# Four gated cross-attention layers with experts: the fourth attention's order of work, its inverse root and its norm

## The chip, the cores and the metric

The kernel runs on one core of a Trainium2 chip, as one launch. The metric is the device time of one execution in microseconds (us). The engines that matter here are TensorE (PE in the profile; its weight loads are PEld), VectorE (DVE), ScalarE (ACT) and GpSimd (POOL); SyncE (SP) issues most of the transfers, GpSimd those whose addresses are computed.

## The reference

The residual x is 16 x 128 rows ("blocks" of 128 tokens) of 256 numbers. Four times it goes through a cross-attention to a context of 128 rows a block and through a feed-forward layer, each behind a layer norm and added back through a gate. All is float32. The change is mostly in the fourth attention, which is followed by the fourth feed-forward layer, a mixture of experts with 8 experts a token:

```python
x = x + jnp.tanh(g_xattn[3]) * _L3_xattn_ref(_layernorm(x, axis=-1), ctx_1024, ...)
x = x + jnp.tanh(g_ffn[3]) * _L3_ffn_ref(_layernorm(x, axis=-1), L3_ffn_router_weight, ...)

# _L3_xattn_ref, 16 heads of 16, EPS = 1e-06, y = context, DCA = 16
y_dca = y[:, -DCA:, :]
y_main = y[:, :-DCA, :]
kv_dca = (y_dca @ Wkv_dca + bkv_dca).reshape(b, DCA, 2, H, HD)
k_dca = _ln(kv_dca[:, :, 0], kn_dca_w, kn_dca_b)
q = _ln((x @ Wq + bq).reshape(b, s1, H, HD), qn_w, qn_b)
k = _ln(kv[..., :HD], kn_w, kn_b)          # kv from y_main
ctx = _attn(qT, k, v)                      # softmax over 112 keys
ctx_dca = _attn(qT, k_dca, v_dca)          # softmax over 16 keys
return (ctx + ctx_dca) @ Wo + bo
```

`_ln` divides each head's 16 deviations from the mean by the root of their variance plus 1e-6: for a block of 128 tokens that is one inverse root for each token, each of the 16 heads, and q and k, an array of 128 x 32. The fourth mixture sends each token to its 8 best of 64 experts; an expert takes the first 128 tokens sent to it.

## The kernel before

Eight stages run one after the other over x, which stays in SBUF as `x_sb`: xattn0, ffn0, xattn1, ffn1, xattn2, ffn2, xattn3, ffn3. The last pair, xattn3 and ffn3, is block 4.

**xattn3.** A step handles one block b of 128 tokens; step n of the loop does the scores and exponentials of block n, the sums and values of block n-1, the output projection of block n-2, and prepares blocks n+2 and n+3. The pieces of a step are these, with the lines in the profile.

- `project_qk` (L1261 to L1265): queries and keys of a block into one PSUM bank; VectorE adds the bias. The weights have had each head's mean taken out, so the results are deviations already. `squares` (L1269) squares them on ScalarE.
- `normalise_qk` (L1273 to L1278): VectorE sums the squares of each head into v (128 x 32), divides by 16 and adds 1e-6; `inverse_root` (L392 to L401) finds 1/sqrt(v) on VectorE from a shifted-integer guess and three Newton steps; GpSimd multiplies q and k by it.
- `turn_qk` (L1287 to L1300): TensorE transposes q and k, ScalarE copies them out with the norm's weights (qT, kT).
- `scores` and `maxima` (L1315, L1327): products of q and k into the four "sc" banks, then eight VectorE reduces that write the negative maximum of each part of the keys beside the queries. `with_maxima` transposes and copies the queries again (qT), and `exponentials` (L1315, L1340) forms the products the other way round, the maximum already taken off, and applies Exp on ScalarE, four times.
- `project_v` (L1345 to L1348): values, on TensorE and ScalarE.
- `add_up` and `values` (L1358, L1364): TensorE sums the exponentials and weights the values; VectorE takes the reciprocal rd of the sums.
- `quotients` (L1376 to L1381): TensorE spreads rd over a bank, ScalarE copies it (rs), VectorE multiplies (aT).
- `project` (L1387, L1388, L410): four matmuls and a fifth with a row of ones for the bias; VectorE adds the gated result to x.

PSUM gives four banks to "sc", two to "tr" (transposes, sums, rd's spread and the router's logits), one to "av" and one to "pj" (both projections).

**The norm and the additions before it.** The rows that the third mixture of experts returned (yg) are added to x block by block (`settle`, L287, four additions a block). `norm_steps` puts the work of a group of four blocks at fixed steps: the four additions-to-x of blocks from eight steps ahead, then statistics (L427 to L430), 1/sqrt on GpSimd (L385), the normalised rows (L442) and their transposition (L455, L463). The first group is done ahead of the loop (`layernorm`).

**The router of the fourth mixture.** The object `head` gets a `done(b)` for each block that leaves `project`, and after each pair of blocks it lays out a list of pieces, one for each following tick; a step has two ticks, one after `quotients` and one at its end. The pieces are: norm statistics, rows, transposition, logits (L158 to L166), the 8 largest (L171 to L176), chosen experts and their weights (L185 to L204), places in the experts' rows (L212), targets (L222 to L234), and then the sends (L240), 16 a pair of blocks, by which GpSimd scatters the rows hx to the experts' buffer `xs_f`, one transfer for each of the 8 choices of each block. `finish`, at the head of ffn3, runs what is left. ffn3 then loads the rows of each expert (xe, L1447), transposes them (L761), and computes.

**What sets the order.** In xattn3 the instructions of TensorE, VectorE and ScalarE run in the order in which the code issues them (`manual_schedule`); those of GpSimd and the transfer queues are ordered by the framework's scheduler. Each engine executes in order, so an instruction that waits holds back all behind it on that engine. The other stages leave all engines to the scheduler, except where they too write the order out. The loop, before:

```python
for b in range(B + 2):
    normalise_qk(b + 2); scores(b); maxima(b, first of 4 banks)
    add_up(b - 1); values(b - 1); maxima(b, other banks)
    project(b - 2); quotients(b - 1)
    tick(done=b - 2)
    with_maxima(b); project_qk(b + 3); exponentials(b); project_v(b)
    squares(b + 3); turn_qk(b + 2); norm work of step b
    tick()
```

Of the kernel before, what the change touches and what calls it, by code (L numbers as in the profile page):

```python
# [28 lines left out]
P = 128  # L29
# [62 lines left out]
class Routed:  # L92
# [30 lines left out]
    def tick(self):  # L123
        self.now += 1
        for f in self.due.pop(self.now, ()):
            f()

    def finish(self):
        self.net.mark = None
        for n in sorted(self.due):  # L130
            for f in self.due[n]:
                f()
        self.due = {}

    def pieces(self, p):
# [8 lines left out]
        def stats():  # L144
            h["stats"] = net.ln_stats(sp, b0, 2)
# [8 lines left out]
        def logits():  # L154
# [7 lines left out]
            nc.vector.tensor_reduce(mx, lg, AX.X, ALU.max)  # L162
            sh = tile("sh", [P, 2, E])
            nc.vector.tensor_tensor(sh, lg, mx.unsqueeze(2).to_broadcast([P, 2, E]), ALU.subtract)

            nc.vector.tensor_scalar(sh, sh, LOWEST, None, ALU.max)  # L166

        def top():
            top, idx, x = tile("top", [P, 2, 8]), tile("idx", [P, 2, 8], U32), h["x"]
            for j in range(2):  # L170
                nc.vector.max(top[:, j, :], h["sh"][:, j, :])  # L171
                nc.vector.max_index(idx[:, j, :], top[:, j, :], h["sh"][:, j, :])
            nc.vector.tensor_copy(x[:, :, D : D + K], idx[:, :, 0:K])
            nc.vector.tensor_copy(x[:, :, D + K : D + 2 * K], self.ids[:, b0 : b0 + 2, :])
            w = tile("w", [P, 2, K])
            nc.scalar.activation(w, top[:, :, 0:K], AF.Exp)  # L176
            if self.over_all:
                nc.scalar.activation(tile("ex", [P, 2, E]), h["sh"], AF.Exp)

        def chosen():  # L180

            m, x = tile("m", [P, 2, E]), h["x"]
            if K == 8:
                for j in range(2):
                    nc.vector.match_replace(m[:, j, :], h["top"][:, j, :], h["sh"][:, j, :], 1.0)  # L185
                nc.vector.tensor_scalar(m, m, 0.5, None, ALU.is_gt)
            else:
                iota = net.cst[:, C_IOTA : C_IOTA + E].unsqueeze(1).to_broadcast([P, 2, E])
                for k in range(K):
                    dst = m if k == 0 else tile("m1", [P, 2, E])  # L190
                    nc.vector.tensor_tensor(dst, x[:, :, D + k : D + k + 1].to_broadcast([P, 2, E]), iota, ALU.is_equal)
                    if k:
                        nc.vector.tensor_tensor(m, m, dst, ALU.add)
            for j in range(2):
                nc.vector.tensor_tensor(
# [3 lines left out]
        def weights():  # L199
            den = tile("den", [P, 2])  # L200
            nc.vector.tensor_reduce(den, h["ex"] if self.over_all else h["w"], AX.X, ALU.add)
            nc.vector.reciprocal(den, den)
            nc.vector.tensor_scalar(den, den, self.gate, None, ALU.mult)
            nc.vector.tensor_tensor(  # L204
# [13 lines left out]
        def targets():  # L218

            pos, m = h["pos"], h["m"]  # L220
            if self.spare:
                nc.vector.scalar_tensor_tensor(m, pos, float(self.room), m, ALU.is_lt, ALU.mult)  # L222
            enc = tile("enc", [P, 2, E])
            base = net.cst[:, self.base : self.base + 2 * E].rearrange("p (b e) -> p b e", b=2)
            nc.vector.tensor_tensor(enc, pos, base, ALU.add)
            nc.vector.tensor_tensor(enc, enc, m, ALU.mult)
            r8 = tile("r8", [P, 2, 8])
            for j in range(2):
                nc.vector.max(r8[:, j, :], enc[:, j, :])
            row = tile("row", [P, 2, K], U32, bufs=4)  # L230
            if self.spare:
                own = tile("own", [P, 2, K])
                nc.vector.tensor_scalar(own, self.ids[:, b0 : b0 + 2, :], float(-self.tiles * P), None, ALU.add)
                nc.vector.tensor_tensor(row, r8, own, ALU.max)  # L234
# [16 lines left out]
        def first():  # L251
            chosen()
            weights()
# [30 lines left out]
    def add(self, b, yg):  # L284
        x = self.net.x[:, b, :]
        for k in range(self.K):
            self.net.nc.vector.tensor_tensor(x, x, yg[:, k, :], ALU.add)  # L287


class Net:  # L290
# [96 lines left out]
    def inverse_root(self, v, n):  # L387
# [3 lines left out]
        half = self.sb(self.small, "half", [P, n], I32)  # L391
        nc.vector.tensor_scalar(half, v.bitcast(I32), 1, None, ALU.logical_shift_right)  # L392
        guess = self.sb(self.small, "guess", [P, n], I32)
        nc.vector.tensor_scalar(guess, half, -1.0, float(0x5F3759DF), ALU.mult, ALU.add)
        y = guess.bitcast(F32)
        for _ in range(3):
            t = self.sb(self.small, "nt", [P, n])
            nc.vector.tensor_tensor(t, y, y, ALU.mult)
            nc.vector.scalar_tensor_tensor(t, t, -0.5, v, ALU.mult, ALU.mult)
            z = self.sb(self.small, "ny", [P, n])  # L400
            nc.vector.scalar_tensor_tensor(z, t, 1.5, y, ALU.add, ALU.mult)  # L401
            y = z
        return y
# [10 lines left out]
    def tick(self, done=None):  # L414

        if self.head is not None:
            if done is not None:
                self.head.done(done)
            self.head.tick()

    def ln_stats(self, pool, b0, n):
# [3 lines left out]
        for i in range(n):  # L425
            st = self.sb(pool, "st", [P, 6])
            nc.vector.bn_stats(st, self.x[:, b0 + i, :])  # L427
            nc.vector.bn_aggr(mv[:, i, :], st)
        ve = self.sb(pool, "ve", [P, n])
# [38 lines left out]
    def layernorm(self, pool, by_expert=False, groups=range(4)):  # L468
        for g in groups:
            self.settle(pool, 4 * g, 4)  # L470
            stats = self.ln_stats(pool, 4 * g, 4)
            for h in range(2):
                b0 = 4 * g + 2 * h
                self.ln_turn(b0, self.ln_rows(pool, b0, stats, 4, 2 * h), by_expert)

    def settle(self, pool, b0, n):

        if self.routed is not None:
            ygs = [self.routed.fetch(pool, b, 2) for b in range(b0, b0 + n)]
            for i, yg in enumerate(ygs):  # L480
                self.routed.add(b0 + i, yg)

    def norm_steps(self, pool, first, every):
# [4 lines left out]
        def at(n, f, *args):  # L488
            steps.setdefault(max(0, n), []).append(partial(f, *args))

        def stats(g, held):
            held["s"] = self.ln_stats(pool, 4 * g, 4)

        def rows(g, h, held):
            held[h] = self.ln_rows(pool, 4 * g + 2 * h, held["s"], 4, 2 * h)
# [1122 lines left out]
```

## Time and profile before

| | us |
|---|---|
| median of 3 executions | 2532.65 |
| lowest, highest | 2532.24, 2535.24 |
| the profiled execution | 2590.16 |
| its span, first to last instruction | 2588.1 |
| PE busy | 2063.5 (80%) |
| DVE busy | 1492.3 (58%) |
| ACT busy | 879.2 (34%) |
| POOL busy | 805.3 (31%) |

The mean granted TensorE clock is 0.916. The profile's page has one row for each group of instructions: the line of the kernel, the engine, the operation, output and inputs, their shape, how many, the busy time and the mean of one in ns, then the idle time of the engine just before them with what ended most of it. A timeline row gives the start in us from the span's start, the duration, the engine, and what the instruction is; in brackets stands the idle time before it and what released it ("issue" where the profile shows nothing that it waited for). xattn3 lies between 1910 us (its first norm) and 2366 us (the last send), ffn3 after it.

### The profile page before, as it was taken

Reading aid. Unit: us, or ns where it says so; the run is one execution under the profiler, and the core shown is the slowest. Engines: PE = TensorE matmul, PEld = TensorE weight load, DVE = VectorE, ACT = ScalarE, POOL = GpSimd, SP = SyncE. Lnnn points to the kernel's source line nnn. Section 1 sums busy time; section 2 is a strip of 40 time slices with the busy share of each in tenths; the row PEclk is TensorE's granted clock in tenths of the full one; section 3 lists DMA queues with packets and bytes.
Section 4 is the critical chain, followed back from the end, with each engine's and each line's share of the span. In section 5 each row is a group of like instructions: output and inputs, shape, how many; then the busy total and the mean of one; then the engine's idle time right before and its main releaser. Section 6 shows DMA issues by size and latency. Waiting matters only on the chain. (4 is left out here: it accounts for less than half of the span.)

```text
span 2588.1 us, 38336 instructions
## 1 busy us (share of the span) xinstructions
PE 2063.5 (80%) x13052; PEld 1423.3 (55%) x13052; DVE 1492.3 (58%) x4196; ACT 879.2 (34%) x1870; POOL 805.3 (31%) x799
## 2 busy tenths in 40 slices
PE   6999998788886878998989988988855878653770
PEld 3767764366664544665666654555534656532550
DVE  2766764478885445667666653454456755332448
ACT  3333333366662224444444431122213333201330
POOL 0221111243542222334444441122231134445340
PEclk9999998899997998999999999999987888766995
DMA  7049961119003760000000021388742001125768
GB/s 233 1 90 247 286 193 33 50 56 350 16 22 117 243 204 5 13 5 32 18 24 18 16 66 57 119 247 247 241 151 74 10 37 55 61 72 177 241 211 292
DMA packets 198567, 299.33 MB, mean 116 GB/s; under 512 B 21295, under 2 KB 151318, under 8 KB 195686
## 3 DMA queue, kind: packets, MB, share of 16 engines
q1 hardware_dynamic: 176102, 238.90, 31.9%
q0 software_dynamic: 19488, 55.31, 5.7%
q10 hardware_dynamic: 2784, 2.68, 0.3%
q8 instruction: 105, 1.72, 0.3%
q14 instruction: 88, 0.72, 0.1%
HBM read 160.92 MB, written 135.90 MB: 115 GB/s over the span
## 5 line engine op out<-in xcount | busy, mean ns | idle before, releaser
L273 POOL DMA_INDIRECT y_f<-ys,drow x182 | 174.1, 957 | 462.1 <-DVE ys L1039 248.4
L543 POOL TENSOR_TENSOR e<-e,r 128x512 f32<-128x512 f32 x128 | 132.7, 1037 | 585.3 <-DVE r L542 310.9
L240 POOL DMA_INDIRECT xs_f<-hx,hrow x224 | 221.4, 988 | 115.6 <-issue 57.3
L531 ACT ACTIVATE e<-e 128x512 f32<-128x512 f32 x128 | 80.7, 630 | 484.5 <-DVE e L528 484.5
L1017 PE MATMUL mm<-wgu,xeT 128*128 128x352 f32 x472 | 168.0, 479 | 7.2 <-DVE xeT L1010 2.9
L761 PE MATMUL tr<-cst,xe 128*128 128x128 f32 x364 | 73.3, 284 | 104.7 <-DMA xe<-xs_f 56.7
L1111 PE MATMUL qk<-wa,xnT 128*128 128x512 f32 x256 | 130.6, 634 | 23.8 <-DVE nq L1125 23.8
L538 DVE TENSOR_REDUCE sm<-e 128x4 f32<-128x512 f32 x128 | 87.8, 686 | 93.5 <-ACT e L531 92.7
L761 PEld LDWEIGHTS tr<-cst,xe 128*128 128x128 f32 x364 | 43.4, 143 | 157.7 <-issue 94.8
L1037 PE MATMUL o<-wdn,hT 88*128 88x256 f32 x472 | 123.5, 384 | 2.1 <-ACT hT L1030 2.1
L643 PE MATMUL y<-wb,aT 128*128 128x256 f32 x512 | 121.1, 379 | 1.0 <-DVE x_sb L410 1.0
L1164 PE MATMUL y<-wb,aT 128*128 128x256 f32 x512 | 120.9, 379 | 0.0
L1021 DVE TENSOR_TENSOR h<-sg,mm 128x176 f32<-128x176 f32 x118 | 39.7, 337 | 139.8 <-issue 89.8
L643 PEld LDWEIGHTS y<-wb,aT 128*128 128x128 f32 x512 | 97.1, 190 | 41.8 <-issue 18.7
L609 PE MATMUL mm<-xnT,wm 128*128 128x512 f32 x256 | 120.1, 593 | 0.0
L385 POOL TENSOR_TENSOR rr<-ss,nhalf 128x8 f32<-128x8 f32 x64 | 105.9, 1654 | 32.7 <-DVE ss L1119 32.6
L287 DVE TENSOR_TENSOR x_sb<-x_sb,yg 128x256 f32<-128x256 f32 x224 | 93.2, 423 | 31.0 <-DMA yg<-y_f 18.3
L1125 DVE TENSOR_TENSOR nq<-qk,rr 128x512 f32<-128x512 f32 x64 | 44.3, 692 | 113.1 <-POOL rr L385 113.1
L1030 ACT COPY hT<-tr 88x256 f32<-88x256 f32 x118 | 43.4, 368 | 190.9 <-PE tr L1028 190.8
L1017 PEld LDWEIGHTS mm<-wgu,xeT 128*128 128x128 f32 x472 | 82.3, 194 | 44.3 <-DVE xeT L1010 15.5
L839 DVE TENSOR_REDUCE mx<-sc 128x4 f32<-128x512 f32 x128 | 84.6, 682 | 37.3 <-PE sc L832 37.3
L516 PEld LDWEIGHTS tr<-cst,e 128*128 128x128 f32 x512 | 63.1, 141 | 72.2 <-issue 58.2
(288 smaller groups left out, 4909.6 us busy)
## 6 DMA issues: line engine op xcount, KB each, us to landing
wgu<-in_L_W SPq DMA_DIRECT2D x118, 352.0 KB
xs_f<-zeros SPq DMA_DIRECT2D x32, 1072.0 KB
wdn<-in_L_W SPq DMA_DIRECT2D x118, 176.0 KB
xs_f<-zeros SPq DMA_DIRECT2D x16, 1048.0 KB
y_f<-zeros SPq DMA_DIRECT2D x16, 1024.0 KB
yg<-y_f SPq DMA_DIRECT2D x16, 1024.0 KB
wgu<-in_L_gu SPq DMA_DIRECT2D x64, 192.0 KB
xe<-xs_f SPq DMA_DIRECT2D x79, 134.0 KB
```

Source lines behind the costliest of these rows:

```text
L240: ins = nc.gpsimd.indirect_dma_start(out=self.rows, out_offset=bass.IndirectOffsetOnAxis(ap=h["row"][:, j, k : k + 1], axis=0), in_=h["x"] ...
L273: self.net.unordered("y_" + self.name, self.net.nc.gpsimd.indirect_dma_start(out=self.y, out_offset=bass.IndirectOffsetOnAxis(ap=row, axis ...
L287: self.net.nc.vector.tensor_tensor(x, x, yg[:, k, :], ALU.add)
L385: return self.nc.gpsimd.tensor_tensor(out, var, self.nhalf[:, :n], ALU.pow)
L543: nc.gpsimd.tensor_tensor(e, e, r.unsqueeze(2).to_broadcast([P, 4, S]), ALU.mult)
L609: nc.tensor.matmul(mm, wm[:, kk, 4 * hq + j, :], self.xnT[:, kk, g * 512 : (g + 1) * 512], start=kk == 0, stop=kk == 1,)
L643: nc.tensor.matmul(y, a[:, j, :], wn[:, 4 * hq + j, :], start=j == 0, stop=j == 3)
L761: self.nc.tensor.transpose(tr[:, kk, :], src[:, kk * P : (kk + 1) * P], self.ident)
L1017: nc.tensor.matmul(gu, xeT[:, kk, :], wgu[:, kk, :], start=kk == 0, stop=kk == 1)
L1037: nc.tensor.matmul(y, hT[:, c, :], wdn[:, c, :], start=c == 0, stop=c == 1)
L1111: nc.tensor.matmul(q, self.xt(kk, b), wq[:, kk, cols], start=kk == 0, stop=kk == 1)
L1164: nc.tensor.matmul(y[b], a[:, j, :], wn[:, h, :], start=h == 0, stop=h == 15)
```

## The change

It has five parts.

1. *Inverse root.* `inverse_root` becomes Ln and Exp(-0.5 ·) on ScalarE, each 128 x 32, and one Newton step on VectorE, three operations. It is split in two: `deviations` sums the squares and issues Ln and Exp; `normalise_qk`, later in the step, does the Newton step and has GpSimd multiply. The scaling and the 1e-6 go into the activation's scale and bias (`eps`), so the VectorE operation for them is gone. `preload_act_table_set` is asked for at the head of the stage.
2. *Order of a step.* All maxima stand ahead of `add_up`; `quotients` and `exponentials` follow `deviations`, `normalise_qk` comes behind them; `project`, `project_qk`, `squares`, `turn_qk` and `project_v` come behind the first tick. `done(b - 2)` is given to the second tick instead of the first. `add_up` takes its bank from "pj" instead of "tr".
3. *Norm by pairs.* The first two pairs of blocks are normed ahead of the loop, the others by `norm_pairs`, one piece at each half step, and these pieces go into the ticks.
4. *Small operations alternate.* The router's pieces, the statistics and the additions of yg become generators that yield after each small VectorE operation; `weave` issues one operation of each piece of a tick in turn. The order of a few operations within a piece changes as well (the 8 largest of both blocks first, then their indices). This is also used in the stages before, in blocks 2 and 3.
5. *Output bias.* The bias row, times the gate, is spread over 128 partitions once (`byrow`); GpSimd adds it to x for each pair of blocks after the norm of that pair has read x, and the fifth matmul of `project` is gone.

The core of the diff:

```diff
     def tick(self):
         self.now += 1
-        for f in self.due.pop(self.now, ()):
-            f()
+        return self.due.pop(self.now, [])
...
+def weave(fs):
+    left = [g for g in [f() for f in fs] if g is not None]
+    while left:
+        left = [g for g in left if next(g, left) is not left]
...
-    def inverse_root(self, v, n):
+    def inverse_root(self, v, n, scale, eps):
         nc = self.nc
-        half = self.sb(self.small, "half", [P, n], I32)
-        nc.vector.tensor_scalar(half, v.bitcast(I32), 1, None, ALU.logical_shift_right)
-        guess = self.sb(self.small, "guess", [P, n], I32)
-        nc.vector.tensor_scalar(guess, half, -1.0, float(0x5F3759DF), ALU.mult, ALU.add)
-        y = guess.bitcast(F32)
-        for _ in range(3):
-            t = self.sb(self.small, "nt", [P, n])
-            nc.vector.tensor_tensor(t, y, y, ALU.mult)
-            nc.vector.scalar_tensor_tensor(t, t, -0.5, v, ALU.mult, ALU.mult)
-            z = self.sb(self.small, "ny", [P, n])
-            nc.vector.scalar_tensor_tensor(z, t, 1.5, y, ALU.add, ALU.mult)
-            y = z
-        return y
+        y = self.sb(self.small, "guess", [P, n])
+        nc.scalar.activation(y, v, AF.Ln, scale=scale, bias=eps[0])
+        nc.scalar.activation(y, y, AF.Exp, scale=-0.5)
+        yield y
+        t = self.sb(self.small, "nt", [P, n])
+        nc.vector.scalar_tensor_tensor(t, v, eps[1] / scale, y, ALU.add, ALU.mult)
+        nc.vector.scalar_tensor_tensor(t, t, -0.5 * scale, y, ALU.mult, ALU.mult)
+        z = self.sb(self.small, "ny", [P, n])
+        nc.vector.scalar_tensor_tensor(z, t, 1.5, y, ALU.add, ALU.mult)
+        yield z
...
-    def tick(self, done=None):
+    def tick(self, done=None, others=()):
         if self.head is not None:
             if done is not None:
                 self.head.done(done)
-            self.head.tick()
+            others = [*others, *self.head.tick()]
+        weave(others)
...
+            pj = self.psum("pj", [P, D])
+            nc.tensor.matmul(pj, self.ones[0:1, :], bo, start=True, stop=True)
+            byrow = self.sb(self.wpool, "wc", [P, D])
+            nc.vector.tensor_scalar(byrow, pj, self.tg[:, 3:4], None, ALU.mult)
+            def add_bias(b0):
+                for b in (b0, b0 + 1):
+                    nc.gpsimd.tensor_tensor(self.x[:, b, :], self.x[:, b, :], byrow, ALU.add)
...
-            def normalise_qk(b):
+            def deviations(b):
                 v = self.sb(self.small, "v32", [P, 32])
                 nc.vector.tensor_reduce(v, sq.pop(b).rearrange("p c (h n) -> p (c h) n", n=16), AX.X, ALU.add)
-                nc.vector.tensor_scalar(v, v, 1.0 / 16.0, 1e-6, ALU.mult, ALU.add)
-                r = self.inverse_root(v, 32)
+                dev[b] = self.inverse_root(v, 32, 1.0 / 16.0, (eps, 1e-6))
+                next(dev[b])
+
+            def normalise_qk(b):
+                r = next(dev.pop(b))
...
             def add_up(b):
-                sm = self.psum("tr", [P, S])
+                sm = self.psum("pj", [P, S])
...
-                    nc.tensor.matmul(y, a[:, c, :], wo4[:, c, :], start=c == 0, stop=False)
-                nc.tensor.matmul(y, self.ones[0:1, :], bo, start=False, stop=True)
+                    nc.tensor.matmul(y, a[:, c, :], wo4[:, c, :], start=c == 0, stop=c == 3)
...
+            def norm_pairs():
+                steps = {}
+                ...
+                for p in range(2, B // 2):
+                    s, held = 2 * p - 3, {}
+                    for i, f in enumerate((
+                        partial(self.settle, sp, 2 * p, int(p > 2)), partial(self.settle, sp, 2 * p + 1, int(p > 2)),
+                        partial(stats, p, held), partial(rows, p, held), partial(turned_rows, p, held),
+                    )):
+                        steps.setdefault(divmod(max(0, 2 * (s - 2) + i), 2), []).append(f)
+                return steps
...
-                self.layernorm(sp, groups=(0,))
-                norm = self.norm_steps(sp, -3, 4)
-                for b in range(3):
+                nc.scalar.preload_act_table_set("natural_log_exp_and_others")
+                self.layernorm(sp, groups=(0,), n=2)
+                for b in range(2):
                     project_qk(b)
                     squares(b)
-                    if b < 2:
-                        normalise_qk(b)
+                self.layernorm(sp, groups=(1,), n=2)
+                for b in range(2):
+                    deviations(b)
+                    normalise_qk(b)
+                project_qk(2)
+                squares(2)
                 turn_qk(0)
                 turn_qk(1)
+                add_bias(0)
+                add_bias(2)
+                weave([partial(self.settle, sp, 4, 2)])
+                norm = norm_pairs()
```

and the loop, after:

```python
for b in range(B + 2):
    now, back, late = b < B, 0 <= b - 1 < B, 0 <= b - 2 < B
    if now:
        banks = scores(b)
        maxima(b, banks, range(4))
    if back:
        add_up(b - 1)
        values(b - 1)
    if now:
        with_maxima(b)
    if b + 2 < B:
        deviations(b + 2)
    if back:
        quotients(b - 1)
    if now:
        exponentials(b)
    if b + 2 < B:
        normalise_qk(b + 2)
    self.tick(None, norm.get((b, 0), ()))
    if late:
        project(b - 2)
    if b + 3 < B:
        project_qk(b + 3)
        squares(b + 3)
    if b + 2 < B:
        turn_qk(b + 2)
    if now:
        project_v(b)
    self.tick(b - 2 if late else None, norm.get((b, 1), ()))
```

## The prediction

> **What bounds the kernel now.** I read the busy time of stages first, then single steps of block 4's attention on the timeline, then GpSimd's groups at its end. The edits that matter lie in that stage; the routed experts before it and after it keep their work.
>
> Busy time by engine in stretches of that stage: prologue, step 0, steps without router sends, steps with them, and the sends after the loop.
>
> ```profile
> core 0: us, PE busy (x) PEld busy (x) DVE busy (x) ACT busy (x) POOL busy (x), PEclk, DMA share, GB/s
> 1910.00:1951.00 41.00, 15.87 (x84) 11.00 (x84) 29.78 (x96) 6.33 (x11) 12.20 (x20) 0.69 0.25 79
> 1951.00:1988.00 37.00, 17.33 (x169) 14.08 (x169) 23.98 (x68) 8.11 (x14) 2.20 (x3) 0.64 0.37 114
> 1988.00:2089.00 101.00, 86.68 (x1054) 70.23 (x1054) 70.29 (x236) 39.70 (x77) 12.31 (x18) 0.90 0.04 13
> 2089.00:2285.00 196.00, 141.12 (x1399) 111.06 (x1398) 86.61 (x319) 51.37 (x101) 85.90 (x95) 0.75 0.16 59
> 2285.00:2366.00 81.00, 23.54 (x184) 17.41 (x183) 20.84 (x105) 6.44 (x14) 47.77 (x50) 0.63 0.25 86
> ```
>
> No engine fills it. Step 0 alone takes 37 us, 16.4 of them VectorE's 40 additions of L287: group 1's norm and blocks up to 10 are settled there. One later step, on the timeline:
>
> ```profile
> 2049.44 0.75 DVE L1327 TENSOR_REDUCE qk<-sc 128x4 f32<-128x448 f32 x2
> 2050.11 0.95 DVE L1364 RECIPROCAL rd<-tr 128x128 f32<-128x128 f32 x1
> 2050.97 2.01 DVE L1327 TENSOR_REDUCE qk<-sc 128x4 f32<-128x448 f32 x6
> 2055.26 0.58 ACT L1378 COPY rs<-tr 128x512 f32<-128x512 f32 x1 [10.62 <-PE tr L1376]
> 2055.88 0.69 DVE L1381 TENSOR_TENSOR aT<-av,rs 128x512 f32<-128x512 f32 x1 [1.27 <-ACT rs L1378]
> 2059.37 2.06 ACT L1340 ACTIVATE e<-sc 128x512 f32<-128x512 f32 x4 [1.24 <-PE sc L1315]
> 2064.47 0.68 DVE L1273 TENSOR_REDUCE v<-sq 128x32 f32<-128x512 f32 x1
> 2067.76 0.75 DVE L1327 TENSOR_REDUCE qk<-sc 128x4 f32<-128x448 f32 x2
> ```
>
> I count steps by M, the end of the maxima (here 2053.0). The quotient aT starts at M+2.9, because rs is ready by then; from there VectorE works nearly without a gap, and the next maxima wait behind the sum v and the inverse root (2064.47 to 2067.8, 3.3 us) although their scores have been ready since 2062.8. M to M is 18.3 us.
>
> The end of the stage is GpSimd's: 48 sends after the loop, and the first expert's load behind the last.
>
> ```profile
> L240 POOL DMA_INDIRECT xs_f<-hx,hrow x48: 956/960/1162, 2304.2 to 2364.5; - x48
> ```
> ```profile
> 2364.53 0.97 POOL L240 DMA_INDIRECT xs_f<-hx,hrow  x1 [0.30 <-issue]
> 2366.98 0.32 SPq L1447 DMA_DIRECT2D xe<-xs_f  x1
> 2369.18 0.29 PEld L761 LDWEIGHTS tr<-cst,xe 128*128 128x128 f32 x2 [45.27 <-issue]
> ```
>
> A send costs 0.96 + 0.30 = 1.27 us. M of step 15 is 2285.0; the last send ends at M15 + 80.5.
>
> **The recorded execution against the median.** It took 2590.16 us, the median is 2532.65: 57.5 more. While sends run, TensorE sometimes falls to one matmul per 0.7 us or longer with nothing to wait for:
>
> ```profile
> 2276.99 0.37 PE L1358 MATMUL tr<-e,wd 128*32 128x128 f32 x1 [0.98 <-issue]
> 2277.68 0.37 PE L1358 MATMUL av<-e,vx 128*32 128x128 f32 x1 [0.32 <-issue]
> 2279.09 0.37 PE L1358 MATMUL av<-e,vx 128*32 128x128 f32 x1 [1.04 <-issue]
> ```
>
> Elsewhere ScalarE stands 15.5 us before e (to 2244.05) although its scores ended at 2229.8. The nine steps with sends average 23.4 us against 18 for those without. I take the 57.5 us as stalls of recording there, by size only: no run shows it yet. Then M0 (1950.9) to the last send (2365.5) is 414.6 recorded and 357 undisturbed, and both versions pay the stalls alike (as many sends).
>
> **Part 1, inverse root.** Removed per step: 11 small VectorE operations at 0.22 = 2.5 us of that 3.3. Added: three at 0.22 = 0.65, and Ln and Exp on ScalarE, 128x32, about 0.25 each (hw, 128x16, takes 0.22). The order of instructions in the built program has more: the preload stands at the start of ScalarE's program, and in block 4 a table load stands before every Ln and another before the Exp after it, 32 in all, where before there was one (the preload's own set is replaced by the layers in between). The row for a load, with what surrounds it:
>
> ```profile
> 825.45 1.28 ACT L1019 ACT_TABLE_LOAD   x1 [17.67 <-PE mm L1017]
> 826.75 0.32 ACT L1019 ACTIVATE sg<-mm 128x176 f32<-128x176 f32 x1
> ```
>
> 1.28 us, and the next activation follows 0.02 later. The Trainium skill, "ScalarE: Activation LUTs", section "Table sets: the hidden batching unit", says that Ln and then Exp cost one load, since one set holds both; by it a step would pay nothing. The instruction order contradicts it for this program. Section "What ACT_TABLE_LOAD costs" gives 1.28 plus 1.38 of draining, 2.66 a switch. The traced pair shows no such drain, so I take 1.29: two loads 2.6 us a step. By the first rule 0, by the second 5.3.
>
> Place: after the query copy qT, before rs and the four e, in ScalarE's order. From M: transposes 0.75, qT to 1.6, load 2.9, Ln 3.2, load 4.5, Exp 4.7, rs 5.3, aT to 6.0. The sum v, which Ln reads, is there at M+1.65, so it is the load and not v that Ln waits for. aT thus starts at M+5.3 where it was M+2.9. Behind it in VectorE's queue stand the Newton step (GpSimd's normalise, the next transposes and TensorE's next scores wait for that), the first tick's router work, the residual add and the next projection's bias add. VectorE's 1.85 us saved lay before the maxima; the 2.6 is added to ScalarE's leg.
>
> **Part 2, new order.** All eight reduces of the maxima now precede the softmax sums; project and project_qk stand behind the first tick and share the single "pj" bank, project_qk behind project in TensorE's queue. So a chain runs aT, tick, residual add, projection, bias add, copies, scores, maxima. In full steps, at full TensorE clock:
> Even: Newton 6.65; tick (first, hx, norm statistics) about 3.3, independent operations overlapping by 0.1, to 9.95; residual add 0.48 to 10.4; projection 1.9 (2055.44 to 2057.33) to 12.4; bias add 13.15; sq, qT, kT 0.6 + 0.75 + 1.0 to 15.5; transpose of hx, which needs kT's bank, 16.2; scores 17.45; maxima 2.76: M' = M + 20.2.
> Odd: xnT copied behind the e's, 8.0; router logits 9.15; tick (targets, softmax start, settle) 2.8 to 11.95; residual add 12.4; projection 14.4; bias add 15.1; second tick (top, statistics, settle) 3.3 to 18.4; maxima: M' = M + 21.2.
> Early and late steps lack parts. Step 0: 13.1; 1: 15.9; 2: 16.5; 3: 16.8; 4: 18.8; 5: 20.4; 6 to 10: 20.2, 21.2, 20.2, 21.2, 20.2; 11: 19.5; 12: 19.0. Sum M0 to M13: 243. TensorE is granted 0.75 to 0.90 here, and about 4 us a step of the chain are its: +1 us a step, 256.
>
> **Part 3, norm by pairs.** It empties step 0: 13 us against 36.9 in the trace (1950.9 to 1987.8); that gain is inside the 243. It spreads settling over steps 0 to 10, where before it was over by step 4. Undisturbed, the late steps before are (196 - 57.5)/8 = 17.3 us, so they lose 2 to 4 each.
>
> **Part 4, the tail.** Router pieces hang on the end tick: pair 4's targets come in step 15, pair 5's in 17, half a step later than before (14, 16). After step 13 GpSimd has 4 + 16 + 64 sends left: 84 x 1.27 = 107, plus rs, the normalise and the start at M13+7.9: M13 + 117, without a gap. Against M15 + 80.5 before, this tail swallows what steps 13 to 15 gain. Inside the loop GpSimd's order is normalise first, then at most five sends ahead of each rs (the norm's power, L385): rs is late by 5 x 1.27 = 6.4 us at most, and the rows xn that follow it are due only for the next step's projection, so nothing of it reaches the chain. Before, 16 sends stood ahead of one such rs (2221.4 to 2241.3), and VectorE waited 10.6 us for it.
>
> **Part 5, the rest.** Prologue: two norms of two blocks and four table loads in one ScalarE line (4 x 1.28 = 5.1), against a smaller first group: M0 later by 4 (between 0 and 8). GpSimd's 16 bias additions, taken at 0.6 each by its normalise row, lie in its idle time (89 of 101 us in the third stretch above, 110 of 196 in the fourth); without that cover they would cost 10 us. The bias matmul L1388 (0.69 a step) goes from a queue that then waits for VectorE: nothing. Alternating small operations in blocks 2 and 3: router pieces there fill gaps of waiting engines, 0 to -3, taken as 0. The preload at the start, 1.28, lies under the input loads.
>
> **Sum.** After: 256 + 117 = 373; before 357: +16; prologue +4: **+20 us**, so 2553 by the median, 2610 by a recorded execution.
>
> **Rivals.**
> *Table loads not on the path (ends faster).* If they hide behind TensorE's second product (1.2 us) and the sum v, or the set stays loaded, 13 steps give back 2.6 each: 33 us, 2520. For: ScalarE is busy only 40 of 101 us. Against: the first load stands behind qT, which ends at M+1.6 while v is there at M+1.65, so nothing is left to hide it behind, and rs stands behind both. With 1.5 us a step hidden (20/13) the sum is even, from 1.9 on (25/13) it is faster by more than a measurement leaves open.
> *The chain is longer (slower still).* TensorE's clock falls with the longer pauses to the 0.64 of step 0, doubling 4 us a step, or the drain is real (2.7 a step): +35 more, 2588.
> *No change.* The emptied step 0 (24 us) and shorter VectorE queue equal the loads: 2533. For: the difference of two sums of about 360 is small.
>
> **Chances.** Forecast 0.55, loads hidden 0.20, longer chain 0.15, no change 0.10. A measurement tells 0.2% (5 us) from nothing. Faster 0.22, within 0.12, slower 0.66. The likeliest case alone spans 2540 to 2572 (1.2 us a step over 13 steps); with the others 2512 to 2590.
>
> **What would show it.** Two table loads of 1.28 in each step between qT and rs; aT about 5.3 us after the maxima; steps of 20 to 21 us between 6 and 10; step 0 near 13; GpSimd without gaps from step 13. Wrong if aT follows the maxima by 3 us, if steps stay below 18, or if sends stop at the loop's end.

## The result: 2541.9 us against 2532.2

After takes 2541.92 us (median), before 2532.23 in the same set of ten executions each. That is 9.7 us more by the medians. The ratio is 1.0043, with a 95% interval of 1.0029 to 1.0056, which is 10.9 us (7 to 14). The forecast was slower by 20, and 2553. One of after's ten executions, 3544.95 us at a granted clock of 0.552, was in a slow state and is left out of the ratio.

The profiled execution of after took 2541.4 us, its span is 2539.6. The first profile of before, on which the prediction rests, took 2590.16. A second profile of the same kernel, taken among the experiments below, took 2540.74 with a span of 2538.6; it is the fairer one to set beside after. The kernels of one set run on one chip beside before. On one of the chips before takes 2587 us in each of its executions (2583 to 2594), 51 more than on another (2536); figures from different chips are therefore compared as ratios to before on the same chip. Even the ratios do not carry over from the chip of 2587: one and the same kernel has 0.9843 there and 0.9895 on another chip (one_load_in_turn and in_turn_again below).

The stages of block 4 in after, in the view of busy time by stretches (columns as in the prediction): prologue, steps 0 to 6, steps 7 to 12, and from M13 to the last send.

```profile
core 0: us, PE busy (x) PEld busy (x) DVE busy (x) ACT busy (x) POOL busy (x), PEclk, DMA share, GB/s
1889.00:1939.00 50.00, 24.53 (x94) 15.58 (x94) 27.38 (x75) 12.56 (x19) 15.15 (x25) 0.57 0.27 91
1939.00:2067.00 128.00, 94.85 (x1184) 76.54 (x1185) 67.57 (x199) 66.99 (x117) 19.34 (x28) 0.86 0.08 26
2067.00:2198.00 131.00, 93.00 (x1068) 74.51 (x1068) 65.83 (x234) 59.09 (x105) 56.91 (x65) 0.84 0.16 57
2198.00:2316.00 118.00, 43.69 (x516) 35.34 (x516) 37.97 (x178) 20.25 (x39) 84.62 (x89) 0.71 0.29 103
```

In steps 0 to 6 TensorE and VectorE are busy for 0.74 and 0.53 of the time, less than in before's steps 1 to 6 (0.86 and 0.70), and ScalarE for 0.52 (0.39 there). One step of after on the timeline; M is the end of the first row, 2133.47:

```profile
2130.73 2.73 DVE L1366 TENSOR_REDUCE qk<-sc 128x4 f32<-128x448 f32 x8
...
2134.22 0.78 ACT L1332 ACTIVATE qT<-tr,n 128x512 f32<-128x512 f32 x1 [3.38 <-PE tr L1326]
2134.25 0.62 DVE L1309 TENSOR_REDUCE v<-sq 128x32 f32<-128x512 f32 x1
2135.01 1.28 ACT L416 ACT_TABLE_LOAD   x1
2136.31 0.32 ACT L416 ACTIVATE guess<-v,eps 128x32 f32<-128x32 f32 x1
2136.64 1.28 ACT L417 ACT_TABLE_LOAD   x1
2137.94 0.23 ACT L417 ACTIVATE guess<-guess 128x32 f32<-128x32 f32 x1
2138.07 0.57 ACT L1417 COPY rs<-tr 128x512 f32<-128x512 f32 x1
2138.67 0.69 DVE L1420 TENSOR_TENSOR aT<-av,rs 128x512 f32<-128x512 f32 x1 [3.80 <-ACT rs L1417]
...
2143.79 0.48 DVE L431 SCALAR_TENSOR_TENSOR x_sb<-pj,tg,x_sb 128x256 f32<-128x256 f32 x1
2148.14 0.69 DVE L1301 TENSOR_TENSOR qk<-pj,bqk 128x512 f32<-128x512 f32 x1 [3.88 <-PE pj L1299]
```

The two loads stand between qT and rs, and VectorE waits 3.80 us for rs: aT starts at M + 5.2. In the second profile of before it starts 0.3 to 1.3 us after the maxima in twelve of the steps 1 to 13, as here (M is 2108.67):

```profile
2106.66 2.01 DVE L1327 TENSOR_REDUCE qk<-sc 128x4 f32<-128x448 f32 x6
...
2108.98 0.68 DVE L1381 TENSOR_TENSOR aT<-av,rs 128x512 f32<-128x512 f32 x1
```

In the groups of the stage after has 16 + 16 loads:

```profile
L416 ACT ACT_TABLE_LOAD x16 | 20.5, 1283 | 0.3
L417 ACT ACT_TABLE_LOAD x16 | 20.5, 1283 | 0.3
```

From 2206 us on GpSimd does 84 sends. It idles 0.3 us ahead of each, and only once longer, 1.5 us for new targets (hrow):

```profile
L257 POOL DMA_INDIRECT xs_f<-hx,hrow x84 | 81.1, 966 | 26.3 <-issue 23.6 <-DVE hrow L251 1.5 <-DMA xs_f<-hx,hrow 1.2
```

Marks of the stage in the profiles of six kernels, in us. "Start" is the first matmul of block 4's setup, M0 and M13 end the maxima of steps 0 and 13, "send" ends the last send. The two profiles of before differ in M0 to send (see before_again).

| | start | start to M0 | M0 to M13 | M13 to send | start to send | send to end |
|---|---|---|---|---|---|---|
| before, first profile | 1907.8 | 43.1 | 272.4 | 142.2 | 457.7 | 222.6 |
| before, second profile | 1906.1 | 45.2 | 243.7 | 118.4 | 407.3 | 225.2 |
| after | 1889.5 | 49.9 | 258.7 | 117.7 | 426.3 | 223.8 |
| one_load | 1894.4 | 45.4 | 227.7 | 114.6 | 387.7 | 223.6 |
| old_root | 1893.9 | 50.2 | 244.9 | 117.8 | 412.9 | 225.9 |
| alternate_only | 1890.7 | 47.0 | 257.1 | 125.1 | 429.1 | 223.7 |

Within the stage after loses 19.0 us (407.3 to 426.3), where the prediction said 20. What it did not say is in the first column: everything ahead of block 4 ends some 17 us sooner in these two profiles.

### The profile page after: what moved, and what is told of

Read it like the earlier page. It is cut to its first block, busy times and chain, and to the rows that moved or that the text cites. A ratio compares the mean times of both kernels' runs of the same rounds, so it can differ in the third digit from the quotient of the medians.

```text
span 2539.6 us, 38214 instructions
## 1 busy us (share of the span) xinstructions
PE 2029.6 (80%) x13022; PEld 1399.3 (55%) x13022; DVE 1448.2 (57%) x4057; ACT 927.0 (37%) x1934; POOL 820.0 (32%) x820
```

## The experiments

Three sets of four kernels. The first (before_again, alternate_only, one_load, old_root) and the third (one_load_again, in_turn_again, all_in_turn, sends_sooner) ran on chips where before takes 2536 us, the second (upstream_only, one_load_in_turn, root_alone, norm_fours) on the one where it takes 2587.

### before_again: the first profile's 57 us

The kernel before, unchanged, profiled once more.

> The kernel before, profiled once more. If the 57.5 us by which its first profiled execution was longer than the median are stalls of recording that come by chance, this execution is well below 2590 us (near 2533 to 2550), the steps with sends (8 to 15) average 17 to 19 us instead of 25, and TensorE has no one-matmul-per-0.7-us stretches there. Rival: the stalls belong to the program; then it takes about 2590 again. Block 4 begins at 1908 us in the first profile of before and at 1889 in that of after: if the 18 us are the change's, it begins at 1908 again; if they too are chance, at about 1890.

It took 2540.74 us. Steps 7 to 12 take 16.2 to 19.3 us, steps 13 and 14 23.0 and 15.9. The stretches of the prologue, step 0, steps without sends, steps with them and the tail in this second profile of before:

```profile
1906.00:1951.00 45.00, 17.70 (x92) 11.62 (x92) 32.03 (x96) 6.34 (x11) 11.06 (x21) 0.72 0.23 78
1951.00:1988.00 37.00, 16.90 (x167) 13.83 (x168) 24.09 (x70) 8.12 (x14) 2.21 (x3) 0.64 0.34 114
1988.00:2089.00 101.00, 86.69 (x1052) 70.10 (x1051) 70.08 (x236) 39.77 (x77) 11.97 (x18) 0.90 0.04 12
2089.00:2234.00 145.00, 113.66 (x1403) 92.71 (x1403) 85.98 (x320) 51.23 (x101) 80.51 (x89) 0.88 0.20 74
2234.00:2313.00 79.00, 22.62 (x183) 17.13 (x181) 20.88 (x104) 6.54 (x14) 53.16 (x56) 0.63 0.28 101
```

The second and third rows are as in the first profile, the fourth is 145 us where it was 196. So the stalls are not the program's alone. They are not a chance of one recording either: the second set shows about 2587 in all of before's 13 executions on its chip, and in all four profiles of that set M13 to the last send takes 140 to 146 us, as in the first profile of before (142.2; 118.4 in the second). They go with that chip. That the first profile comes from it is not on record and is inferred from these marks. M0 to the last send is 362.1 undisturbed; the prediction took 357. And block 4 starts at 1906.1 again, which speaks for the earlier start of after being the change's; upstream_only and all_in_turn test it by timing.

### alternate_only: one part of five alone

After's generators and `weave` in every block, with the new order of a few operations within a piece, but block 4's attention as it was (order, root, norm, bias).

```diff
-    def xattn3(self): ... as in after
+    def xattn3(self): ... as in before
+                    for f in norm.get(b, ()):
+                        weave([f])
```

> Only the alternating of small VectorE operations and the new order of a few of them, in all blocks; block 4's attention keeps its order, root, norm and bias of before. By the prediction's term this is worth 0 to -3 us: 2530 to 2533. By the gap between the two profiles (block 4 begins 18 us earlier in after) it is worth up to -18: about 2515.

2545.63 us, ratio 1.0034 (1.0022 to 1.0045): 8.6 us slower, which neither figure had. Block 4 starts 15.4 us sooner, and then takes 21.8 more (429.1 against 407.3), steps 6, 8, 10 and 12 with 21 to 23 us each where they were 17.7 to 18.6. The timeline of one such step:

```profile
2101.30 0.28 DVE L234 SCALAR_TENSOR_TENSOR hm<-tr,hm 128x128 f32<-128x128 f32 x1
...
2102.66 0.60 PE L1314 MATMUL tr<-cst,qk 128*128 128x128 f32 x4
2105.89 1.09 PE L1314 MATMUL tr<-cst,qk 128*128 128x128 f32 x4 [2.63 <-ACT qT L1320]
2108.09 1.12 PE L483 MATMUL tr<-cst,xn 128*128 128x128 f32 x4 [1.11 <-ACT kT L1327]
2109.88 1.97 PE L157 MATMUL tr<-wrf,xnT 128*128 128x64 f32 x8 [0.67 <-ACT xnT L491]
2111.89 0.29 DVE L161 TENSOR_REDUCE hmx<-tr 128x2 f32<-128x128 f32 x1 [10.31 <-PE tr L157]
2112.10 0.28 DVE L238 TENSOR_TENSOR henc<-tr,cst 128x128 f32<-128x128 f32 x1
```

The targets' first operation (L234) runs at 2101.30. Its second, L238, is the last to read that "tr" bank, and it now stands behind L161 of the logits piece, which waits 10.31 us for TensorE. So one of the two "tr" banks is held for 11 us (2101.30 to 2112.38), and the transposes of q, k and xn and the logits go through the other one, each waiting for ScalarE's copy of the one ahead. In the second profile of before the same eight transposes of q and k run as one row (2114.47, 1.04 us). Alternating a piece that waits with one that is ready lengthens what the ready one holds.

### upstream_only: the same, alternating ahead of block 4 alone

```diff
+IN_TURN = [False]          # True from the start of xattn3 on
 def weave(fs):
+    if IN_TURN[0]:
+        for f in fs:
+            for _ in f() or ():
+                pass
+        return
```

> As alternate_only, but in block 4's attention the small operations are issued in turn, piece after piece, as before; they alternate in the blocks ahead of it alone. If alternating gains 16 us ahead of block 4 (it begins at 1890 us against 1906) and loses 22 within it (a bank of transposes is held by the targets, which wait behind the logits of the next pair), this takes 16 us less than before: 0.9935, about 2520, with odd steps of 16 to 18 us again. If the gain ahead of block 4 is only between two profiles, it takes what before takes.

Ratio 0.997 (0.9955 to 0.9986), on the chip of 2587 us: 7.7 us less (4 to 12), half of what was expected, with the step times of before's first profile, within 0.3 us each but for step 6 (18.9 against 17.7). So the loss within block 4 goes with the alternating there, and the gain ahead of it is real and smaller than the two profiles made it. The new order of operations within a piece is part of this gain.

### one_load: the table loads taken off

```diff
-                nc.scalar.preload_act_table_set("natural_log_exp_and_others")
+                last = nc.scalar.copy(self.sb(one, "last", [P, 1]), bqk[:, 0, 0:1])
+                tables = nc.scalar.preload_act_table_set("natural_log_exp_and_others")
+                self.tc.add_manual_dep(tables.ins, last.ins.name, NO_SYNC, reason="behind the other sets")
```

The preload depends on nothing, so in after it stands at the head of ScalarE's program and is replaced by other sets before block 4. Tied behind an activation of block 4's setup it stays in its place, and no other load follows until ffn3.

> The kernel after with the preload of the set that holds both Ln and Exp tied behind the last activation ahead of block 4's attention; the program then has one table load in the stage instead of 32. If the loads stand on the path of each step as forecast (2 x 1.29 us, 14 loop steps and some in the prologue), it takes 33 to 40 us less than after: 2502 to 2509, with aT about 2.7 us after the maxima and full steps near 19.5 us instead of 22. Rival, the loads are hidden: within 5 us of after, 2537 to 2547.

2507.02 us, ratio 0.9883 (0.9861 to 0.9904); once more in the third set, 0.9874 (0.9858 to 0.989). Against after (1.0043) that is 1.6%, about 40 us; the bare medians, which come from different sets, differ by 34.9. The step of the timeline above, in one_load:

```profile
2106.89 2.73 DVE L1366 TENSOR_REDUCE qk<-sc 128x4 f32<-128x448 f32 x8
...
2110.38 0.78 ACT L1332 ACTIVATE qT<-tr,n 128x512 f32<-128x512 f32 x1 [3.38 <-PE tr L1326]
2111.07 0.32 ACT L416 ACTIVATE guess<-v,eps 128x32 f32<-128x32 f32 x1
2111.42 0.23 ACT L417 ACTIVATE guess<-guess 128x32 f32<-128x32 f32 x1
2111.74 0.59 ACT L1417 COPY rs<-tr 128x512 f32<-128x512 f32 x1
2112.36 0.69 DVE L1420 TENSOR_TENSOR aT<-av,rs 128x512 f32<-128x512 f32 x1 [1.32 <-ACT rs L1417]
```

The loads are gone and aT starts at M + 2.73 (3.45 to 3.68 in every second step from step 7 on). Start to send is 38.6 us shorter, as the ratios have it: M0 to M13 31.0 (13 steps of 2.4), the prologue 4.5, the tail 3.1. The 26 loads from M0 to M13 take 33.4 us, so nearly all of their time was on the path.

### old_root: after's order without Ln and Exp

```diff
-        nc.scalar.activation(y, v, AF.Ln, scale=scale, bias=eps[0])
-        nc.scalar.activation(y, y, AF.Exp, scale=-0.5)
-        yield y
-        t = ...                                # one Newton step
+        nc.vector.tensor_scalar(v, v, scale, eps[1], ALU.mult, ALU.add)
+        yield v
+        half = ...                             # the guess and three Newton steps of before
...
-                nc.scalar.preload_act_table_set("natural_log_exp_and_others")
```

> The kernel after with the former inverse root (a shifted-integer guess and three Newton steps on VectorE) at the place of the one Newton step: no Ln, no Exp of the root, no table load in the loop; nine more small VectorE operations a step. aT then starts near M+2.9 instead of M+5.2, and the root ends near M+6.2 instead of M+6.65: about 0.5 us a step, 6 to 10 us less than after in all (2532 to 2536), if the chain through VectorE is as worked out. Rival: VectorE's queue is the bound of a step and nine operations at 0.22 cost 2 us each step: 2560 or more.

2534.3 us, ratio 1.000 (0.9987 to 1.0013): as forecast, and 0.4% less than after (10.9 us; 7.6 by the bare medians). aT starts at M + 2.7 to 3.5; what comes behind it is later by the nine operations. On the same chip the same order with the new root and one load (one_load) takes 27 us less, so the short root is worth that much here, and the loads took more than all of it.

### root_alone: the new root in before's order

Before, with the new `inverse_root` at its old place ahead of the maxima and the preload tied as in one_load; nothing else.

```diff
-                nc.vector.tensor_scalar(v, v, 1.0 / 16.0, 1e-6, ALU.mult, ALU.add)
-                r = self.inverse_root(v, 32)
+                for r in self.inverse_root(v, 32, 1.0 / 16.0, (eps, 1e-6)):
+                    pass
```

> Before with the new inverse root alone, at its old place ahead of the maxima, and one table load for the stage: VectorE's 3.3 us from v to the maxima become about 1.9 (v 0.7, Ln 0.3, Exp 0.2, three operations 0.65). Where the next maxima wait for VectorE, that is 1.4 us in each of up to 16 steps and the prologue: 10 to 22 us less, 2514 to 2526. Rival: TensorE or ScalarE is as late in most steps, and it takes what before takes within 5 us.

Ratio 0.9947 (0.9928 to 0.9967), 13.7 us less on the chip of 2587 us: within what was expected. Steps 0 to 6 are 0.3 to 1.8 us shorter than those of upstream_only on that chip.

### one_load_in_turn, in_turn_again, all_in_turn: what alternating is worth

one_load with `weave` issuing piece after piece in block 4 (the edit of upstream_only); once more on the chip of one_load_again; and with piece after piece in every block.

> As one_load, but in block 4's attention the small operations are issued in turn. If alternating costs there what it cost in the order of before (some 1.5 us a step), about 2487. If in the new order no transposition waits for the held bank, the overlap of the small operations is lost instead, up to 1 us a tick in full steps: 2515 to 2525.

> one_load once more, on the chip of the three runs beside it, as their measure: 0.983 to 0.990 of before.

> one_load_in_turn once more, beside one_load on one chip. If alternating in block 4's attention is worth nothing in the new order (M0 to M7 took 107.5 us in turn and 106.8 alternating), within 6 us of one_load. If it costs there what it cost in the order of before, 15 to 20 us less than one_load; if it gains up to 1 us a tick, 10 to 20 us more.

> As in_turn_again, but with the small operations in turn in every block, those ahead of block 4 too. The difference to in_turn_again is what alternating is worth there: by the starts of block 4 in the profiles (1890 to 1897 us against 1906 to 1908) 10 to 17 us more than in_turn_again; by the timing of upstream_only about 8; by the prediction 0 to 3.

| | ratio to before, same chip | 95% interval | median us |
|---|---|---|---|
| one_load_in_turn | 0.9843 | 0.9828 to 0.9857 | 2546.31 (of 2587.28) |
| one_load_again | 0.9874 | 0.9858 to 0.9890 | 2505.58 |
| in_turn_again | 0.9895 | 0.9878 to 0.9913 | 2511.77 |
| all_in_turn | 0.9912 | 0.9897 to 0.9928 | 2515.92 |

The first row has its own chip, where one_load did not run, and tells nothing of the alternating. It is the kernel of in_turn_again, and the two intervals do not meet: this is the evidence that ratios of the chip of 2587 do not carry over. Of the last three, on one chip, in_turn_again and one_load_again can't be told apart: in the new order no cost or gain of alternating in block 4 can be told from noise, and start to send is 389.4 and 389.5 in their profiles. all_in_turn against in_turn_again is 4.2 us, with overlapping intervals. Their steps from M0 to M15 are the same within 0.1 us (13.3, 13.6, 13.7, 15.2, ... in both), so what differs lies ahead of block 4, which starts at 1899.0 and 1888.4 in their profiles; the execution behind the second was 7.4 us under its median.

Over all profiles that were made, block 4 starts at 1905.1 on average without alternating ahead of it (4 profiles, 1899.0 to 1907.8) and at 1894.7 with it (10 profiles, 1888.4 to 1903.1): 10.4 us. The starts of kernels that are alike up to there differ by up to 15 us, so this is a rough figure. Timing gives 4 (all_in_turn, the alternating alone) and 8 (upstream_only, with the new order within a piece). A part of it shows in the attention of block 3, in TensorE's wait for kT, in before (second profile) and after:

```profile
L1144 PE MATMUL sc<-kT,qT 128*128 128x128 f32 x512 | 71.7, 283 | 21.3 <-ACT kT L1137 21.2
```
```profile
L1169 PE MATMUL sc<-kT,qT 128*128 128x128 f32 x512 | 71.7, 283 | 17.2 <-ACT kT L1162 17.2
```

That is 4.1 us. It is not all the alternating's: all_in_turn, which has the new order within a piece but issues piece after piece, lies between before and its neighbour in_turn_again, which alternates there.

```profile
L1178 PE MATMUL sc<-kT,qT 128*128 128x128 f32 x512 | 72.4, 285 | 19.6 <-ACT kT L1171 19.5
```
```profile
L1178 PE MATMUL sc<-kT,qT 128*128 128x128 f32 x512 | 71.7, 283 | 17.6 <-ACT kT L1171 17.5
```

By these rows of single profiles 2.0 us go with the alternating and 1.7 with the order within a piece. Where the rest of the gain lies stays open.

### norm_fours: step 0 filled again

one_load with the norm by groups of four at before's steps.

```diff
+            def norm_fours():
+                steps = self.norm_steps(sp, -3, 4)
+                for g in range(1, 4):
+                    for h in range(2):
+                        steps.setdefault(max(0, -3 + 4 * g - 3 + h), []).append(partial(add_bias, 4 * g + 2 * h))
+                return steps
...
+                    for f in norm.get(b, ()):
+                        weave([f])
```

> As one_load, but the norm and the additions ahead of it by groups of four blocks at their former steps (the bias additions follow the rows). Step 0 takes 30 to 37 us again instead of 13.3; later steps lose the additions and statistics from their ticks, 1 to 2 us each in steps 5 to 12. By the prediction's account (24 us gained in step 0, 2 to 4 us a step lost behind it) it is within 8 us of one_load: 2507 to 2515. Rival: spreading costs nothing since the ticks have room, and all of step 0's 20 us shows: 2525 or more.

Ratio 0.9911 (0.9894 to 0.9929) on the chip of 2587 us; step 0 takes 37.3 us. The kernel one_load did not run on this chip; against its ratios from the other chips (0.9874 and 0.9883) the figure would be 7 to 9 us more, but ratios do not carry over. Against one_load_in_turn on the same chip (0.9843), which differs in the alternating as well, it is 17.6 more, nearer to the rival. There M0 to M13 is 255.6 against 234.9: step 0 is 24.0 us longer, steps 1 to 4 are 0.8 to 3.4 longer, steps 5 to 12 on average 1.6 shorter (nearly half of it in step 7, 17.1 against 22.9). Pairs are better than fours, by some 18 us on this chip; what they are worth on the others was not measured.

### sends_sooner: the tail

```diff
-        many = 4 if K == 8 else 1
+        many = 8 if K == 8 else 1
...
+        def top_first():
+            yield from top()
+            first()
+        tops = [top_first] if K == 8 else [top, first]
-        return [stats, rows, turn, logits, top, first, places, targets, *sends]
+        return [stats, rows, turn, logits, *tops, places, targets, *sends]
```

> As one_load, but the 8 largest and the chosen experts of a pair fall in one tick, so its targets come half a step sooner, and the sends go eight a tick instead of four. If GpSimd's sends set the end from step 13 on (M13 to the last send 114 to 118 us in every version on an undisturbed chip), some 8 sends fewer are left then: 5 to 10 us less than one_load. Rival: the tick that holds both pieces, or a norm's power that waits behind more sends, delays the steps: 5 to 15 us more.

2502.72 us, ratio 0.9861 (0.984 to 0.9881): 2.9 us under one_load_again, with overlapping intervals. M13 to the last send stays 114.1, and start to send is 383.0 against 389.5; steps 8, 10 and 12 take 22 to 24 us, those between 17. Four sends fewer are left after M13 (80 for 84), but twice GpSimd now idles 2.8 us or more before a send. Of the gain that was expected there, 0.7 us came; most of the 6.5 us in the profiles lies ahead of M13 (4.1), and why is not shown.

## Why the prediction was right, and where it was off

**Bound and part 1, right to the tenth.** Two loads of 1.283 us in each step between qT and rs, aT at M + 5.21 to 5.27 (predicted 5.3). The step of before in the prediction, with aT at M + 2.9, was not typical, though: 0.3 to 1.3 us is the rule there. So of the later start only 2.5 us are the loads'; the rest is the new order's, in which aT starts at M + 2.7 without loads too (one_load, old_root). The sum did not rest on the comparison, as it was built up from M. The next activation follows a load by 0.02 us (2136.29 to 2136.31), so the 1.38 us of draining in the Trainium skill, "ScalarE: Activation LUTs", section "What ACT_TABLE_LOAD costs", does not show here. The rival of a longer chain thus lost its second leg; the first, a clock falling to 0.64, did not come true either (0.84 to 0.86). The rule of that page's "Table sets: the hidden batching unit", one load for Ln and then Exp, holds where the set is in place (one_load: one load for the stage). The rival that the loads are hidden fell: taking them off shortened M0 to M13 by 31.0 us, where its price for these 13 steps was put at 33. (From the root go twelve VectorE operations, not eleven, the scaling of L1274 among them; at 0.22 us this is 0.2 a step.)

**Part 2, right.** M0 to M13 takes 258.7 us (predicted 256). Steps 6 to 10 average 22.1 (20.6 + 1 for the clock predicted). The difference of 1 us that was worked out between even and odd steps is not there (21.9, then 22.2 four times). Single steps were off by up to 3.7 us (step 5: 21.4 with the clock's 1, measured 17.7) and cancel in the sum; that it is right within 3 us is in part luck.

**Part 3, step 0 right, its price too high.** Step 0 takes 13.6 us (13.1). That the late steps lose 2 to 4 us each for it was too much: norm_fours has it at 1.6 in steps 5 to 12, with steps 1 to 4 the better for pairs. The prediction's reading of step 0 in before was off as well: it has 32 additions of L287 (13.4 us), not 40 (16.4), and it settles eight blocks, 4 to 11. That did not enter the sum.

**Part 4, right.** M13 to the last send is 117.7 (117), with one gap of 1.5 us. In one_load and old_root it is 114.6 and 117.8, so there what steps 13 to 17 gain is swallowed, and what the steps up to 13 gain is kept. Before has nearly the same, 118.4, but for another reason: fewer sends are left then, and GpSimd twice stands still for targets, 17.5 us in all. From 2195 us on in its second profile:

```profile
L240 POOL DMA_INDIRECT xs_f<-hx,hrow x79 | 76.2, 965 | 40.9 <-issue 22.4 <-DVE hrow L234 17.5 <-DVE before L195 0.3
```

That the two tails are equal is a coincidence.

**Prologue.** 4.7 us longer than in the second profile of before (predicted 4).

**The base: the cause was wrong, the size nearly right.** The 57.5 us were put down to recording. They go with one chip, where every execution of before takes as long. Taking them off gave 357 for before where an undisturbed profile shows 362.1, because the median, to which they were taken off, is that of undisturbed executions. "2610 by a recorded execution" was 2541.4. (The steps with sends average 24.5 us in the first profile, 196 over eight, and not 23.4; this had no weight.)

**The term that was mis-sized: part 5, "Alternating small operations in blocks 2 and 3: ... 0 to -3, taken as 0".** It is 4 and 8 us by timing and 10.4 over all profiles. Within the stage the sum came out at +19.0, +20 having been forecast, while after as a whole lost half of that: what is missing is this gain ahead of block 4. 19.0 less 4 to 10 is 9 to 15; measured were 9.7 by the medians and 10.9 by the ratio, so the rival of no change fell too. (The two profiled executions alone differ by only 1.0 us in their spans: 19.0 less 16.6 for the start of block 4 and 1.4 behind the last send. Before's was 4.7 over the median of its chip.) The term was taken at nothing because the pieces seemed to fill gaps of waiting engines. TensorE's wait for kT in block 3, 21.3 us before and 17.2 after, speaks for some of them having stood in TensorE's way; which ones stays open.

The other terms of part 5, the bias additions and the bias matmul taken off, have no run of their own. The 16 additions take 0.73 us each in after (0.6 forecast), and nothing in the profile waits for them.

**Version that beats both.** one_load: 0.9874 and 0.9883 of before. sends_sooner may be another 0.1% under it.

## What to carry to other kernels

Look up in the built order of instructions where a table load lands: the preload without a dependence moved to the head of this program and was worth nothing there, and tied in its place it took off 31 of 32 loads and about 40 us. Work out a stage from its last fixed chain backwards: here GpSimd's sends made M13 plus 114 to 120 us the end in each version with the new order on an undisturbed chip, so only steps ahead of that count. Take more than one step of before as the measure: aT at M + 2.9 was the exception. Alternating independent small operations can gain, but not where one that waits stands among those whose operands hold a bank.

## What the runs showed that was not expected

The same program takes 2532 us in the set of the result, 2536 on two chips and 2587 on a third. The difference lies in the steps in which GpSimd sends: M0 to the last send is 414.6 us in the first profile of before and 362.1 in the second, with the prologue and steps 0 to 6 equal within 2.1 us together. In the profile of one_load_in_turn, on the third chip, matmuls that end near 2188 and 2196 us have their semaphore events (the signals that release waiting engines) 6 and 17 us later; the first profile of before has such delays of up to 11 us, while in block 4's attention of before's second profile, after, one_load_again and in_turn_again none is over 2 us. The disturbed profiles also hold 108 to 134 fewer of these events than matmuls that send one, the others at most 2 more or fewer. Whether the chip does it, or recording on that chip, or the hour at which it ran, stays open.
